# Attention's softmax sums: seven steps of a chunk summed on TensorE

## The chip, the cores and the metric

The kernel runs on one core of a Trainium2 chip. A core has four engines that compute, each with its own queue of instructions: TensorE (PE in the profile; its weight loads are shown apart as PEld), VectorE (DVE), ScalarE (ACT) and GpSimd (POOL). SyncE (SP) issues most DMA transfers. The engines wait for each other through semaphores. TensorE writes its results into PSUM, a memory of banks, and the other engines read them there. The metric is the device time of one execution in microseconds; the time before is the median of three runs.

## What is computed

The reference is a network of two layers on two images of 96 channels and 96 x 96 positions. Layer 0 is a scan with a small feed-forward net, and layer 1 is an attention with another feed-forward net. The change lies in layer 1's attention alone:

```
attn = jnp.einsum('bhdn,bhdm->bhnm', k, q_samp) * scale
attn = jax.nn.softmax(attn, axis=-2)
distribution = jnp.einsum('bhdn,bhnm->bhdm', v, attn)
```

There are 3 heads of 32 channels, n runs over 9216 tokens (keys and values), and m over 2304 cells (queries). The softmax runs over the tokens: for each head and cell, the exponentials of all 9216 scores are summed, and the weighted sum of the values is divided by that sum.

## The kernel before

Layer 1 handles the two images one after the other: a planned stage makes keys, queries and values, `_l1_attention` computes the attention, and a second planned stage makes the output. `_l1_attention` has two arms, chosen by a bound on the scores; in the profile it is the arm without shifted scores, `_l1_packed`, that runs.

`_l1_packed` cuts the 2304 cells into five chunks: four of 480 cells (10 rows of 48) and one of 384. The 9216 tokens are 72 blocks of 128. TensorE's array has 4 strips of 32 rows, and 3 heads fill only three of them, so the fourth strip is given a quarter of the work: 18 of the 72 blocks (`SHARED`), for each of the three heads in turn. What remains is 54 steps for each chunk. In step j, strips 0 to 2 take token block 18 + j of heads 0 to 2, and strip 3 takes block t of head p, where p, t = divmod(j, 18).

One step consists of these pieces:

- Scores (L1311): four matmuls of 32 rows by 128 columns, one for each strip, into two PSUM tiles of two banks (`sc`). There are three such tiles, and a step takes two. The scores of step j + 1 are issued ahead of the values of step j.
- Exponentials (L1315): two ScalarE instructions, each over two strips, into `pr`, of which there are three buffers.
- Values (L1372): four matmuls of 128 rows by 32 columns, which add into a PSUM bank. Strips 0 to 2 write partitions 0 to 95 of the chunk's bank, `main`. Strip 3 writes partitions 96 to 127 of `banks[(m + p) % 2]`, which is the other bank while p is 1.
- Sums (L1380, L1382, L1383, L1385): VectorE adds `pr`, 128 x 4 x 480, into `sums` of the same shape. After 18 steps the fourth strip's part is folded into its head's (L1387), and ScalarE saves its values (L1389).

When a chunk is done, `close` finishes it in three pieces, which are spread over the next chunk. ScalarE first copies the bank (L1325). In step 2 of the next chunk TensorE sums `sums` over the partitions by matmuls with ones (L1328), into the chunk's own bank, and VectorE takes reciprocals (L1332). In step 6 TensorE puts the values back together with the fourth strip's parts (L1336, a matmul of 128 rows, and L1340, one of 32 rows), and VectorE multiplies them into `dist` (L1344). The last chunk's close has no next chunk beside it.

TensorE's order is that of the program (`_in_order`). The other engines' order is left to the scheduler, which puts the reciprocal after the sums of step 3 and the multiplication after those of step 7. An f32 matmul shows as two records of TensorE in the profile, and likewise two weight loads.

Of the kernel before, what the change touches and what calls it, by code (L numbers as in the profile page):

```python
# [8 lines left out]
F32 = mybir.dt.float32  # L9
# [4 lines left out]
ALU = mybir.AluOpType  # L14
# [11 lines left out]
C = 96  # L26
# [17 lines left out]
HEADS = 3  # L44
HD = 32
# [10 lines left out]
def _in_order(k, tc, start, engines=ENGINES):  # L56

    last = {}
    for i in k.nc.cur_bb.bb.instructions[start:]:
        if i.engine in engines:  # L60
            if i.engine in last:
                tc.add_manual_dep(
                    i,
                    last[i.engine].name,
                    mybir.DependencyInfo(
                        mybir.DependencyClass.NoSync, mybir.DependencyReason.DATA
                    ),
                    reason="in_order",
                )
            last[i.engine] = i  # L70
# [1209 lines left out]
SHARED = NTOK // 128 // 4  # L1280


def _l1_packed(k, tc, wk, ps, pa, M):

    nc = k.nc
    qH, kH, vT, dist = M.qH, M.kH, M.vT, M.dist
    steps = NTOK // 128 - SHARED  # L1290
    last = slice(HEADS * HD, (HEADS + 1) * HD)
    chunks = [(r0, min(10, CELLS - r0)) for r0 in range(0, CELLS, 10)]
    banks = [pa.tile([128, 512], F32, tag=f"a{n}", name=f"av{n}", bufs=1) for n in range(2)]
    cells = lambda m: slice(chunks[m][0] * CELLS, (chunks[m][0] + chunks[m][1]) * CELLS)
    q3 = {}

    def load(m, p):
        if m < len(chunks):
            n = chunks[m][1] * CELLS
            q3[m, p] = wk.tile([128, 480], F32, tag="q3", name="q3", bufs=2)  # L1300
            nc.sync.dma_start(q3[m, p][last, :n], qH[p * HD : (p + 1) * HD, cells(m)])

    def scores(m, j):
        n, (p, t) = chunks[m][1] * CELLS, divmod(j, SHARED)
        pr = wk.tile([128, 4, 480], F32, tag="pr", name="pr", bufs=3)
        two = [ps.tile([128, 2, 512], F32, tag="s", name="sc", bufs=3) for _ in range(2)]
        for s in range(4):
            rows = slice(s * HD, (s + 1) * HD)
            k0 = (SHARED + j) * 128 if s < HEADS else (p * SHARED + t) * 128
            q = qH[rows, cells(m)] if s < HEADS else q3[m, p][rows, :n]  # L1310
            nc.tensor.matmul(  # L1311
                two[s // 2][:, s % 2, :n], kH[rows, k0 : k0 + 128], q, start=True, stop=True
            )
        for i in range(2):
            nc.scalar.activation(  # L1315
                pr[:, 2 * i : 2 * i + 2, :n], two[i][:, :, :n], AF.Exp, scale=HD**-0.5
            )
        return pr

    def close(m, av, sums, av3):  # L1320

        n = chunks[m][1] * CELLS
        avs = wk.tile([128, 480], F32, tag="avs", name="avs", bufs=2)
        rden = wk.tile([C, 480], F32, tag="rden", name="rden", bufs=1)
        nc.scalar.copy(avs[:, :n], av[:, :n])  # L1325
        yield
        for hd in range(HEADS):
            nc.tensor.matmul(  # L1328
                av[hd * HD : (hd + 1) * HD, :n], k.ones[:, :HD], sums[:, hd, :n],
                start=True, stop=True,  # L1330
            )
        nc.vector.reciprocal(rden[:, :n], av[:C, :n])  # L1332
        yield
        for hd in range(HEADS):
            rows = slice(hd * HD, (hd + 1) * HD)
            nc.tensor.matmul(  # L1336
                av[rows, :n], k.join[:, rows], avs[:, :n], start=True, stop=hd == HEADS - 1
            )
            if hd < HEADS - 1:
                nc.tensor.matmul(  # L1340
                    av[rows, :n], k.ident[last, last], av3[last, hd, :n], start=False, stop=True
                )
        r0, rows = chunks[m]
        nc.vector.tensor_tensor(  # L1344
            dist[:, 1 + r0 : 1 + r0 + rows, 1 : CELLS + 1],
            av[:C, :n].rearrange("p (r w) -> p r w", w=CELLS),
            rden[:, :n].rearrange("p (r w) -> p r w", w=CELLS),
            ALU.mult,
        )
        yield  # L1350

    start = len(nc.cur_bb.bb.instructions)
    load(0, 0)
    load(0, 1)
    ahead, rest = scores(0, 0), None
    for m in range(len(chunks)):
        n = chunks[m][1] * CELLS
        sums = wk.tile([128, 4, 480], F32, tag="sums", name="sums", bufs=2)
        av3 = wk.tile([128, 2, 480], F32, tag="av3", name="av3", bufs=2)
        for j in range(steps):  # L1360
            p, t = divmod(j, SHARED)
            pr = ahead
            if j + 1 < steps:
                ahead = scores(m, j + 1)
            elif m + 1 < len(chunks):
                ahead = scores(m + 1, 0)
            main, other = banks[m % 2], banks[(m + p) % 2]
            for s in range(4):
                blk, hd = (SHARED + j, s) if s < HEADS else (t, p)
                end = steps if s < HEADS else SHARED  # L1370
                at = j if s < HEADS else t
                nc.tensor.matmul(  # L1372
                    (main if s < HEADS else other)[s * HD : (s + 1) * HD, :n],
                    vT[:, blk, hd, :],
                    pr[:, s, :n],
                    start=at == 0,
                    stop=at == end - 1,
                )
            if j == 0:
                nc.vector.tensor_copy(sums[:, :, :n], pr[:, :, :n])  # L1380
            elif t == 0:
                nc.vector.tensor_tensor(sums[:, :3, :n], sums[:, :3, :n], pr[:, :3, :n], ALU.add)  # L1382
                nc.vector.tensor_copy(sums[:, 3, :n], pr[:, 3, :n])  # L1383
            else:
                nc.vector.tensor_tensor(sums[:, :, :n], sums[:, :, :n], pr[:, :, :n], ALU.add)  # L1385
            if t == SHARED - 1:
                nc.vector.tensor_tensor(sums[:, p, :n], sums[:, p, :n], sums[:, 3, :n], ALU.add)  # L1387
                if p < 2:
                    nc.scalar.copy(av3[last, p, :n], other[last, :n])  # L1389
            if t == 1:  # L1390

                load(m + (p + 2) // 3, (p + 2) % 3) if j > 1 or m else load(0, 2)
            if rest and j in (2, 6):
                next(rest)
        rest = close(m, main, sums, av3)
        next(rest)
    for _ in rest:
        pass
    _in_order(k, tc, start, (mybir.EngineType.PE,))


def _l1_attention(k, tc, M):
# [4 lines left out]
    with ExitStack() as st:  # L1407
# [34 lines left out]
        with cmp.Else():  # L1442
            arm(lambda wk, ps, pa: _l1_packed(k, tc, wk, ps, pa, M), False)
# [363 lines left out]
```

## Time and profile before

| what | value |
| --- | --- |
| time, median of 3 runs | 9239.88 us (9234.12 to 9240.49) |
| profiled execution, its own time | 9236.83 us |
| its span, first to last instruction | 9235.0 us |
| busy: VectorE / TensorE / GpSimd / ScalarE | 8357.2 / 7773.2 / 6272.5 / 6152.4 us |
| attention of the first image | 7129 to 7753 us |
| attention of the second image | 8225 to 8850 us |

The numbers below are from one profiled execution, whose span starts at 0. A group's line gives the code line, engine, operation, output and inputs, shape and count; then the busy time and the mean length of one instruction in ns; then the idle time of the engine just ahead of these instructions and what ended it. Busy time is no measure of a bound by itself, because an engine can be busy while nobody waits for it, and TensorE's records overlap. In attention, windows of 120 us in mid-stage look like this (stretch, its length, busy time and count of TensorE, weight loads, VectorE, ScalarE and GpSimd, then the granted TensorE clock, the DMA share and GB/s):

```profile
7250.00:7370.00 120.00, 119.64 (x840) 36.86 (x836) 114.52 (x59) 95.57 (x106) 0.00 (x0) 1.00 0.01 2
7370.00:7490.00 120.00, 119.63 (x846) 36.75 (x840) 114.78 (x60) 95.51 (x107) 0.00 (x0) 1.00 0.01 3
```

VectorE's busy time leaves a gap of about 0.1 us between two of its instructions where the second waits for a semaphore. TensorE appears busy throughout, which here is the overlap of its records and not a sign that it has no room.

### The profile page before, as it was taken

The page shows a single profiled execution, that of the slowest core. Times are in us where ns is not written, and L with a number is a line of the kernel's source. Part 1 is how long each engine was busy: PE and PEld are TensorE (multiplying, and loading weights), DVE is VectorE, ACT ScalarE, POOL GpSimd, SP SyncE. Part 2 cuts the span into 40 slices and gives each one's busy share as a digit, 9 for nine tenths or more (in the row PEclk, how much of TensorE's full clock was granted, in tenths as well). Part 3 has the DMA queues.
Part 4 walks back from the last instruction along what each step waited for, and adds up shares of the span by engine and source line. Part 5 has one row for each costly group of instructions (what it writes and reads, how often), then busy time and mean ns, then how long its engine had stood idle before and what let it go on. Part 6 is the DMA issues. An engine that isn't in the chain of part 4 may idle for free. (4 is left out here: it accounts for less than half of the span.)

```text
span 9235.0 us, 108247 instructions
## 1 busy us (share of the span) xinstructions
PE 7773.2 (84%) x36625; PEld 3146.3 (34%) x36625; DVE 8357.2 (90%) x6239; ACT 6152.4 (67%) x9970; POOL 6272.5 (68%) x4058
## 2 busy tenths in 40 slices
PE   6888888888888888888888888888857999989998
PEld 3333333333333333333333333333313334543345
DVE  3999999999999999999999999999996998969997
ACT  4666666666666666666666666666645875577755
POOL 4988888888888888888888888888863001210022
PEclk8888888888888888888888888888856999989999
DMA  2444444444444444444444444444431000000000
GB/s 80 131 140 139 140 141 137 136 139 135 134 140 137 134 141 139 139 141 136 138 139 134 135 141 136 136 140 138 137 127 42 3 2 7 20 27 2 2 11 21
DMA packets 335626, 968.69 MB, mean 105 GB/s; under 512 B 50424, under 2 KB 52144, under 8 KB 334768
## 3 DMA queue, kind: packets, MB, share of 16 engines
q1 hardware_dynamic: 335056, 961.64, 32.8%
q8 instruction: 291, 4.77, 0.2%
q14 instruction: 279, 2.29, 0.1%
HBM read 788.04 MB, written 132.17 MB: 100 GB/s over the span
## 5 line engine op out<-in xcount | busy, mean ns | idle before, releaser
L986 POOL TENSOR_TENSOR h<-h,cre 128x864 f32<-128x864 f32 x2048 | 4123.3, 2023 | 806.5 <-DVE h L983 426.7
L983 DVE TENSOR_TENSOR_SCAN h<-dA,bp 128x864 f32<-128x864 f32 x2048 | 4000.0, 1953 | 242.7 <-PE y L995 10.8
L959 ACT ACTIVATE dA<-dlr,A 128x576 f32<-128x576 f32 x3072 | 2156.4, 765 | 1035.0 <-DVE h L983 916.3
L973 DVE TENSOR_TENSOR bp<-dur,B 128x864 f32<-128x864 f32 x2048 | 2174.6, 1062 | 193.4 <-DMA dur<-du_d 11.8
L995 PE MATMUL y<-h,fold 128*32 128x288 f32 x12288 | 2081.1, 592 | 100.3 <-POOL h L986 93.0
L531 PE MATMUL pc<-xin,off 96*96 96x288 f32 x4608 | 1360.2, 427 | 1.6 <-ACT fh L816 1.0
L970 PE MATMUL B<-bt,selb 128*128 128x288 bf16 x2048 | 653.2, 319 | 779.1 <-DVE bp L973 772.2
L1315 ACT ACTIVATE pr<-sc 128x960 f32<-128x960 f32 (+1 forms) x1080 | 955.4, 937 | 255.8 <-DVE sums L1385 144.2
L1385 DVE TENSOR_TENSOR sums<-sums,pr 128x1920 f32<-128x1920 f32 (+1 forms) x510 | 1059.2, 2077 | 58.4 <-ACT pr L1315 7.5
L531 PEld LDWEIGHTS pc<-xin,off 96*96 96x96 f32 x4608 | 743.6, 171 | 575.3 <-issue 281.4
L1466 POOL MEMSET vch<- 96x32 f32 x16 | 2.0, 125 | 1317.4 <-DVE dist L1344 1267.6
L995 PEld LDWEIGHTS y<-h,fold 128*32 128x32 f32 x12288 | 338.9, 116 | 1274.8 <-issue 662.5
L1311 PE MATMUL sc<-qH,kH 32*128 32x480 f32 (+1 forms) x3240 | 708.4, 602 | 9.4 <-DMA q<-qH 9.4
L970 PEld LDWEIGHTS <-selb 128*128 128x128 bf16 x2048 | 205.4, 100 | 1095.1 <-issue 1011.0
L1311 PE MATMUL sc<-q,kH 32*128 32x480 f32 (+1 forms) x1080 | 564.3, 602 | 0.0
L1372 PE MATMUL av<-pr,vT 128*32 128x480 f32 (+1 forms) x4320 | 533.4, 564 | 3.8 <-ACT av L1389 3.5
L705 PE MATMUL pt<-xd,w_dt 96*128 96x288 f32 x768 | 365.7, 573 | 149.7 <-DVE rest L650 88.1
L1311 PEld LDWEIGHTS sc<-qH,kH 32*128 32x128 f32 x3240 | 284.6, 184 | 438.3 <-issue 303.6
L710 ACT ACTIVATE e<-pt,dt_b 128x288 f32<-128x288 f32 x384 | 190.8, 497 | 351.1 <-PE pt L705 341.7
L1539 DVE SCALAR_TENSOR_TENSOR acc<-vch,lepe_w,acc 96x1152 f32<-96x1152 f32 x256 | 406.6, 1588 | 5.0
L1509 POOL TENSOR_TENSOR e<-e,mask 100x384 f32<-100x384 f32 x96 | 146.2, 1544 | 269.3 <-ACT e L1507 269.3
L705 PEld LDWEIGHTS pt<-xd,w_dt 96*128 96x128 f32 x768 | 163.7, 251 | 412.2 <-DVE rest L650 168.0
(249 smaller groups left out, 10476.4 us busy)
## 6 DMA issues: line engine op xcount, KB each, us to landing
cre<-c_d SPq DMA_DIRECT2D x1024, 288.0 KB
dur<-du_d SPq DMA_DIRECT2D x256, 864.0 KB
dlr<-dl_d SPq DMA_DIRECT2D x256, 864.0 KB
x<-xs SPq DMA_DIRECT2D x512, 72.0 KB
du_d<-du SPq DMA_DIRECT2D x128, 288.0 KB
dl_d<-dl SPq DMA_DIRECT2D x128, 288.0 KB
du_d<-du SPq DMA_DIRECT2D x128, 144.0 KB
dl_d<-dl SPq DMA_DIRECT2D x128, 144.0 KB
```

The source lines that it names most:

```text
L531: pe(H2, lambda: nc.tensor.matmul(pc.ap[:C, :H2], k.w_c1[:, ih, tap, oh * C : (oh + 1) * C], xin.ap[:, ih, 3 * c + dy : 3 * c + dy + 3, dx ...
L705: pe(H2, lambda: nc.tensor.matmul(pt.ap[:, :H2], k.w_dt[:, o, m, :], xd.ap[:, cols], start=True, stop=True), ((xd, c),), (pt,), (e, r))
L959: S.op("act", 0.76, lambda blk=blk: nc.scalar.activation(dA.ap[:, :, blk, :], dlr.ap[:, blk, :].rearrange("p (c n) -> p c n", c=2), AF.Exp ...
L970: S.op("pe", 0.3, lambda: nc.tensor.matmul(pB.ap[:, :H2], k.selb[:, kk, i, :], f.bc[o].ap[:, toks], start=True, stop=True), (f.bc[o],), (p ...
L973: S.op("dve", 1.13, lambda: nc.vector.tensor_tensor(bp.ap[:, : NBL * H2].rearrange("p (b n) -> p b n", b=NBL), dur.ap[:, :, toks], pB.ap[: ...
L983: nc.vector.tensor_tensor_scan(hv, dv, bv, 0.0, ALU.mult, ALU.add)
L986: S.op("pool", 2.1, lambda: nc.gpsimd.tensor_tensor(ht.ap, ht.ap, cre.ap[:, toks].unsqueeze(1).to_broadcast([128, NBL, H2]), ALU.mult), (c ...
L995: nc.tensor.matmul(py[c].ap[CB * blk : CB * blk + CB, :H2], k.fold, hv, start=False, stop=(o == 1 and kk == 1 and i == NQ - 1))
L1311: nc.tensor.matmul(two[s // 2][:, s % 2, :n], kH[rows, k0 : k0 + 128], q, start=True, stop=True)
L1315: nc.scalar.activation(pr[:, 2 * i : 2 * i + 2, :n], two[i][:, :, :n], AF.Exp, scale=HD**-0.5)
L1372: nc.tensor.matmul((main if s < HEADS else other)[s * HD : (s + 1) * HD, :n], vT[:, blk, hd, :], pr[:, s, :n], start=at == 0, stop=at == e ...
L1385: nc.vector.tensor_tensor(sums[:, :, :n], sums[:, :, :n], pr[:, :, :n], ALU.add)
```

## The change

In steps 9, 15, 23, 29, 33, 41 and 47 of each chunk VectorE no longer adds strips 0 to 2. Instead TensorE multiplies the exponentials of these three strips by ones, which sums them over the 128 tokens of the block, and adds the result up in partitions 0 to 95 of the bank that the next chunk will use for its values (`side`). VectorE adds only the fourth strip's 480 columns in these steps. After step 47 ScalarE copies the sums from the bank to `part`. At the chunk's close each of the three matmuls by ones is followed by one with a 32 x 32 piece of the identity, which adds `part` to the same partitions.

```diff
+SUMMED = (9, 15, 23, 29, 33, 41, 47)
...
-    def close(m, av, sums, av3):
+    def close(m, av, sums, av3, part):
...
         for hd in range(HEADS):
+            rows = slice(hd * HD, (hd + 1) * HD)
             nc.tensor.matmul(
-                av[hd * HD : (hd + 1) * HD, :n], k.ones[:, :HD], sums[:, hd, :n],
-                start=True, stop=True,
+                av[rows, :n], k.ones[:, :HD], sums[:, hd, :n], start=True, stop=False
+            )
+            nc.tensor.matmul(
+                av[rows, :n], k.ident[rows, rows], part[rows, :n], start=False, stop=True
             )
         nc.vector.reciprocal(rden[:, :n], av[:C, :n])
...
+        part = wk.tile([C, 480], F32, tag="part", name="part", bufs=1)
         for j in range(steps):
...
-            if j == 0:
+            if j in SUMMED:
+                side = banks[(m + 1) % 2]
+                for s in range(HEADS):
+                    nc.tensor.matmul(
+                        side[s * HD : (s + 1) * HD, :n], k.ones[:, :HD], pr[:, s, :n],
+                        start=j == SUMMED[0], stop=j == SUMMED[-1],
+                    )
+                nc.vector.tensor_tensor(sums[:, 3, :n], sums[:, 3, :n], pr[:, 3, :n], ALU.add)
+                if j == SUMMED[-1]:
+                    nc.scalar.copy(part[:, :n], side[:C, :n])
+            elif j == 0:
                 nc.vector.tensor_copy(sums[:, :, :n], pr[:, :, :n])
...
-        rest = close(m, main, sums, av3)
+        rest = close(m, main, sums, av3, part)
```

## The prediction

> **What bounds the kernel now.** I read the page first (busy shares, the chain that ended last, the costly groups), then the windows and the timeline of the two attention stages, then the chain inside one of them. The change touches only attention, which the timeline puts at 7129 to 7753 us (first image) and 8225 to 8850 us (second): some 1,250 of 9235 us.
>
> ```profile
> DVE 29%; PE 14%; issue 2%; ACT 1%; POOL 1%; DVEq 0%; DMA 0%; SPq 0%; POOLq 0%; ACTq 0%
> ...
> L1315 ACT ACTIVATE pr<-sc 128x960 f32<-128x960 f32 (+1 forms) x1080 | 955.4, 937 | 255.8 <-DVE sums L1385 144.2
> L1385 DVE TENSOR_TENSOR sums<-sums,pr 128x1920 f32<-128x1920 f32 (+1 forms) x510 | 1059.2, 2077 | 58.4 <-ACT pr L1315 7.5
> ```
>
> VectorE's running sum of the exponentials (L1385) is busy 1059 us, most of attention, and waits 7.5 us for its input; ScalarE, which makes that input, waits 144 us for L1385 to give a `pr` buffer back. The chain of waits, cut to the middle of a chunk, is that one line (start, length, what):
>
> ```profile
> 7304.48 2.17 DVE sums L1385
> ...
> 7306.74 2.17 DVE sums L1385
> 7308.91 0.03 issue
> 7308.94 0.02 DVEq L1385
> 7308.96 0.04 issue
> 7309.00 2.17 DVE sums L1385
> ```
>
> A step is 2.26 us there, all VectorE's. The question is how far behind TensorE is. That shows where VectorE does not yet hold the ring, right after the first start (TensorE alone, start and length):
>
> ```profile
> 7143.51 1.01 PE L1372 MATMUL av<-pr,vT 128*32 128x480 f32 x8
> 7144.45 0.68 PE L1311 MATMUL sc<-qH,kH 32*128 32x480 f32 x3
> ...
> 7145.47 1.01 PE L1372 MATMUL av<-pr,vT 128*32 128x480 f32 x8
> 7146.41 0.85 PE L1311 MATMUL sc<-qH,kH 32*128 32x480 f32 x3
> 7146.61 0.67 PE L1311 MATMUL sc<-q,kH 32*128 32x480 f32 x1
> ...
> 7147.60 1.01 PE L1372 MATMUL av<-pr,vT 128*32 128x480 f32 x8
> ```
>
> From one value group (L1372) to the next it is 1.96, then 2.13 us, alternating: 0.94 for the values, 1.02 for the scores, and in every second step 0.2 more for the last two score strips, which wait for a score bank that ScalarE still reads. So TensorE and ScalarE together need 2.045 us a step, only 0.22 below VectorE. In the last chunk (384 cells) the same steps take 1.64 and 1.82, mean 1.73, against 1.86.
>
> The third view is a chunk's close, TensorE alone:
>
> ```profile
> 7260.78 0.98 PE L1328 MATMUL av<-sums,ones 128*32 128x480 f32 x6
> 7261.69 0.68 PE L1311 MATMUL sc<-qH,kH 32*128 32x480 f32 x3
> ...
> 7269.76 0.97 PE L1336 MATMUL av<-avs,join 128*32 128x480 f32 x2
> 7270.66 0.99 PE L1340 MATMUL av<-av,ident 32*32 32x480 f32 x2
> 7271.58 0.99 PE L1336 MATMUL av<-avs,join 128*32 128x480 f32 x2
> ```
>
> Three sums by ones (L1328, x6 since an f32 matmul is two records) run beside each other: 0.91 us for all. But where a 128-row matmul and a 32-row identity alternate (L1336, L1340), each one alone takes 0.92.
>
> [...] after a 3.7 us idle the granted clock of 7741 to 7753 is 0.50.
>
> **The change part by part**, one image, against the profiled execution (9236.8 us, span 9235.0, which lies 3.1 below the median of 9239.9).
>
> (a) VectorE, in 7 steps a chunk: an add of 1920 becomes one of 480. L1387 is that form, 0.66; 2.16 - 0.66 = 1.5 us, 10.5 a chunk.
>
> (b) TensorE, in the same steps: three sums by ones after the values, the shape of L1328. Values to scores takes 0.94 without and 1.74 with them (7259.95 to 7261.69), so +0.80; 5.6 a chunk. With 384 columns I estimate 0.64 (0.80 by the column ratio). No new wait ahead of them: they read what the values read, and the bank's last reader (L1344 of the chunk before) ends in step 7 or 8, ahead of step 9.
>
> (c) TensorE, at each close: ones, identity, ones, identity, ones, identity. By the L1336/L1340 row that is 6 x 0.92 = 5.5 in place of 0.80: +4.7. Bounds: +0.8 if the columns ran beside each other, +5.5 if every group were as slow as the slowest.
>
> (d) ScalarE: one copy of 96x480 after step 47, 0.55 by L1389. It waits for the new sums, and the next exponential behind it waits for scores that TensorE issues only after those, about 1.0 us long: hidden, nothing. If that cover were gone, 0.55 a chunk. SP's loads do not move.
>
> Once the 7 adds are gone VectorE needs about 126 - 10.5 = 115 us a chunk and TensorE becomes the bound everywhere. By stretches of steps, from the starts of L1372 in the timeline (chunk 1 as the model of 1 to 3), before and after:
> - 0 to 2: 4.53, then 4.26.
> - 2 to 6, with the first close: 9.0, then 13.7 by (c).
> - 6 to 9, with the second close: 10.5, unchanged.
> - 9 to 17, 2 summed steps: 17.2, then 8 x 2.045 + 2 x 0.80 = 18.0.
> - 17 to 36, 3 summed: 43.5, then 19 x 2.045 + 3 x 0.80 + 0.1 = 41.35 (0.1, an estimate, for the wait at ScalarE's copy L1389).
> - 36 to 54, 2 summed: 41.2, then 18 x 2.045 + 1.6 + 0.2 = 38.65.
> Sum 125.9 before, 126.45 after: +0.5, three times +1.5.
> First chunk, no close: +0.95 - 2.15 - 2.55 = -3.75. Last chunk, 384 cells, with chunk 3's close of 480: stretches 102.75 before; after, 3.5 + 12.4 + 9.6 + 15.1 + 34.9 + 30.9 = 106.4: +3.65.
> At the end VectorE is 2.2 us behind ScalarE now (last `pr` ends 7736.24, its add starts 7738.46). After step 47 it has caught up and loses 0.13 a step for 6 steps, so it is 0.8 behind: -1.5. The last close lies bare: L1328 now takes 1.96 (7740.37 to 7742.33) with the clock falling in it. With TensorE idle only some 2 us before it I expect full clock, 6 x 0.76 = 4.6 (0.92 less 96 columns' share): +2.6. Bounds: at half clock, where L1336 has 1.42 each, 8.5 and so +6.5; if the clock also held through L1336/L1340, 5 x (1.42 - 0.76) = 3.3 would come back, -0.7.
> Sum for an image: -3.75 + 1.5 + 3.65 - 1.5 + 2.6 = +2.5; both images +5. So 9236.8 + 5 = 9242 by the profiled execution, 9244 to 9245 by the median; I take 9244. VectorE's 2 x 48 us of saved adds is nearly all covered by TensorE, which stood 10 us a chunk behind and is given 10.3.
>
> **Rivals.**
> Faster: the closing pairs of different columns run beside each other in spite of the shape. Then (c) costs about 0.9 and not 4.7 at four closes and 2 less at the bare one: 17 us an image, 34 in all, about 9210. For it: the operands are in different columns. Against: L1340 and the following L1336 are too, and show 0.92.
> The change does not do what it says, that is, VectorE stays the bound and its 10.5 a chunk come through in full: 2 x 4.8 x 10.5 = 101 less, 9139. It needs TensorE well under 2.0 us a step; the unblocked step of 1.96 speaks against.
> Slower: TensorE's alternation is lost. Each summed step shifts ScalarE against the score banks (three tiles, two a step). If this makes every step a blocked one (2.13 and 1.82), it costs 0.085 in each of 540 steps, 46 us: 9290. It decides once two steps in three are blocked instead of one in two (15 us on top of the 5). For it: the bound is this very loop. Against: a summed step gives ScalarE 0.8 us to empty its queue, so the following scores should find their banks free.
>
> **How the numbers follow.** A measurement here can tell about 0.2% (18 us) from no change. My case, TensorE takes over at nearly the old pace: 0.70; its own range is 9228 to 9260 (0.5 us a chunk either way is 5, the bare close from -0.7 to +6.5 makes -7 to +8 for two). The closing pairs overlap, 0.12. VectorE stays the bound, 0.02. Lost alternation, or a stall of like size by the 5.5 us close, after which VectorE owes a 3.1 us reciprocal, 0.16. Hence faster 0.14, same 0.70, slower 0.16. The range, widened into both sides, is 9216 to 9270.
>
> **What would show it.** Right: L1315's wait for the sums nearly gone; value groups 2.0 to 2.15 apart with 2.75 to 2.95 at summed steps; six closing groups 0.92 apart; VectorE's adds waiting for ScalarE at most steps; in the chain, TensorE's lines in place of VectorE's. Wrong: closing groups starting within a few ns of each other; summed steps above 3 us; nearly all steps at 2.13; or VectorE still without a pause.

## The result and the profile after

The changed kernel takes 9242.97 us, the median of 12 runs (9240.54 to 9245.44), and the kernel before 9237.44 us beside it (12 runs, 9234.12 to 9240.98). The ratio is 1.0006, with a 95% interval of 0.9997 to 1.0015: the change makes no difference that can be told from none. VectorE has 70 wide additions turned into short ones, and the time stays where it was.

The profile shows that the two kernels get there in different ways. From the page after, the costly groups that answer to those shown of before (line, engine, operation, tiles, shape, count, then busy time and mean length, then the engine's idle time ahead of them and who ended it):

```profile
L1319 ACT ACTIVATE pr<-sc 128x960 f32<-128x960 f32 (+1 forms) x1080 | 954.0, 937 | 255.6 <-PE sc L1315 227.5
L1403 DVE TENSOR_TENSOR sums<-sums,pr 128x1920 f32<-128x1920 f32 (+1 forms) x440 | 913.9, 2077 | 134.3 <-ACT pr L1319 102.6
```

L1319 and L1403 are L1315 and L1385 of before. VectorE's wide sums lost 145 us of busy time (the 70 short adds bring 45 back), and they now wait 103 us for ScalarE where it was 7.5. ScalarE's idle time is the same 256 us as before, but it ended mostly with VectorE's sums (144 us) and now ends with TensorE's scores (228 us). VectorE has gone off the path and TensorE is on it. The chain of waits over the close of a chunk says so line by line (start, length, what):

```profile
7252.78 0.94 PE av L1380 x8
7253.73 1.02 PE sc L1315 x8
7254.74 0.94 PE av L1380 x8
7255.69 0.79 PE av L1333 x2
7256.47 0.92 PE av L1336 x2
7257.39 0.92 PE av L1333 x2
7258.31 0.92 PE av L1336 x2
7259.23 0.92 PE av L1333 x2
7260.15 0.92 PE av L1336 x2
7261.07 1.02 PE sc L1315 x8
```

Every piece is TensorE's. The six groups of the close (L1333 by ones, L1336 by the identity) stand one after the other and take 5.4 us, where three matmuls by ones took 0.91 before. The same chain a few steps on shows a summed step, of values, sums and scores:

```profile
7309.43 0.94 PE av L1380 x8
7310.37 0.80 PE av L1390 x6
7311.17 1.02 PE sc L1315 x8
7312.19 0.94 PE av L1380 x8
7313.13 1.19 PE sc L1315 x8
```

The sums of a summed step (L1390) are 0.80 us, and the steps around them alternate between 1.96 (0.94 + 1.02) and 2.13 us, as they did before where VectorE did not yet hold back the ring of three `pr` buffers. Windows over the same stretches of time as before, with the same columns, show where VectorE's work went:

```profile
7250.00:7370.00 120.00, 119.64 (x882) 31.52 (x876) 103.99 (x59) 94.84 (x107) 0.00 (x0) 1.00 0.01 2
7370.00:7490.00 120.00, 119.64 (x880) 31.76 (x880) 104.97 (x59) 95.22 (x106) 0.00 (x0) 1.00 0.01 3
```

VectorE falls from 114.5 and 114.8 to 104.0 and 105.0 us busy, ten less. TensorE issues 4 to 5% more matmuls in the same time. Its busy time reads 119.6 in both kernels, so that column could not have told who sets the pace.

At the end of an image the close is bare. TensorE's timeline there, before, then after:

```profile
7740.37 1.96 PE L1328 MATMUL av<-sums,ones 128*32 128x384 f32 x6 [3.23 <-DVE sums L1385]
7745.04 1.49 PE L1336 MATMUL av<-avs,join 128*32 128x384 f32 x2 [2.71 <-DVE rden L1332]
7746.46 1.48 PE L1340 MATMUL av<-av,ident 32*32 32x384 f32 x2
```

```profile
7738.57 0.80 PE L1333 MATMUL av<-sums,ones 128*32 128x384 f32 x2 [1.59 <-DVE sums L1403]
7739.30 0.83 PE L1336 MATMUL av<-part,ident 32*32 32x384 f32 x2
7740.06 0.83 PE L1333 MATMUL av<-sums,ones 128*32 128x384 f32 x2
```

TensorE waits 1.59 us for VectorE's last sums instead of 3.23, because VectorE is no longer two microseconds behind. The six groups then run 0.76 apart, at a granted clock of 1.00 (7737 to 7744 us). From the first of them to the reciprocal it is 4.7 us (7738.57 to 7743.27), against 2.07 before (7740.37 to 7742.44).

From the first scores to the end of the last `dist`, attention is 3.7 us longer in the first image and 1.4 in the second. The first two steps run while the clock is still low (granted 0.50 to 0.52 over the first 8 us), and took 1.2 us more in one image and 1.2 less in the other. Without them it is 2.5 us for each image.

### The profile page after: what moved, and what is told of

It reads as the page before. It is cut to its first block, busy times and chain, and to the rows that moved or that the text cites. A ratio compares the mean times of both kernels' runs of the same rounds, so it can differ in the third digit from the quotient of the medians.

```text
span 9238.9 us, 109217 instructions
## 1 busy us (share of the span) xinstructions
PE 7764.9 (84%) x37105; PEld 3096.5 (34%) x37105; DVE 8260.3 (89%) x6239; ACT 6156.3 (67%) x9980; POOL 6269.0 (68%) x4058
## 4 chain that ended last, share of the span: by engine, by line
DVE 61%; PE 26%; issue 5%; ACT 2%; POOL 1%; DVEq 1%; DMA 0%; SPq 0%; POOLq 0%
DVE h L983 34%; DVE bp L973 20%; PE sc L1315 6%; PE av L1380 5%; DVE acc L1557 3%; PE y L995 3%; PE pc L531 3%; DVE rd L1541 1%; PE pp L1573 1%; PE px L603 1%; PE B L970 1%; DVEq L983 1%; PE av L1390 1%; DVE rest L650 1%; POOL h L986 1%
## 5 line engine op out<-in xcount | busy, mean ns | idle before, releaser
L1319 ACT ACTIVATE pr<-sc 128x960 f32<-128x960 f32 (+1 forms) x1080 | 954.0, 937 | 255.6 <-PE sc L1315 227.5
L1403 DVE TENSOR_TENSOR sums<-sums,pr 128x1920 f32<-128x1920 f32 (+1 forms) x440 | 913.9, 2077 | 134.3 <-ACT pr L1319 102.6
L1315 PE MATMUL sc<-qH,kH 32*128 32x480 f32 (+1 forms) x3240 | 622.1, 602 | 10.0 <-DMA q<-qH 10.0
L1315 PE MATMUL sc<-q,kH 32*128 32x480 f32 (+1 forms) x1080 | 564.7, 603 | 0.0
L1315 PEld LDWEIGHTS sc<-qH,kH 32*128 32x128 f32 x3240 | 214.7, 185 | 422.3 <-PE sc L1315 208.5
```

Source lines behind the costliest of these rows:

```text
L1315: nc.tensor.matmul(two[s // 2][:, s % 2, :n], kH[rows, k0 : k0 + 128], q, start=True, stop=True)
L1319: nc.scalar.activation(pr[:, 2 * i : 2 * i + 2, :n], two[i][:, :, :n], AF.Exp, scale=HD**-0.5)
```

## The experiments

All ratios are to the kernel before, which ran beside each group of kernels; its median was 9234.35 us beside `e1_grouped` to `e4_four` and 9235.13 beside `e5_close_only` to `e8_join_before`.

**Is the close slow because of its order?** `e1_grouped` puts the three sums by ones first and the identities after them:

```diff
         for hd in range(HEADS):
             rows = slice(hd * HD, (hd + 1) * HD)
             nc.tensor.matmul(
                 av[rows, :n], k.ones[:, :HD], sums[:, hd, :n], start=True, stop=False
             )
+        for hd in range(HEADS):
+            rows = slice(hd * HD, (hd + 1) * HD)
             nc.tensor.matmul(
```

> The changed kernel with the close's six matmuls in another order: the three sums by ones first, then the three identity pieces. Theory A ([...] six groups of 0.92 us were an effect of the order): ones 0.8 and identities about 0.9 us, 1.7 instead of 5.5 us a close, 3.8 less at four closes and about 3 at the bare one: 18 us an image, 36 in all, so about 9207 us (ratio to before 0.9967). Theory B (a 32-row identity matmul takes 0.92 by itself in any order): 0.8 + 2.8 = 3.6 us a close, 1.9 less at ten closes: about 9224 us. Theory C (the close is covered, and the time has another cause): 9243 us, no change.

Measured: 9205.6 us, ratio 0.9969 (0.9956 to 0.9981). Its close in TensorE's timeline:

```profile
7257.05 0.98 PE L1333 MATMUL av<-sums,ones 128*32 128x480 f32 x6
7257.96 1.00 PE L1338 MATMUL av<-part,ident 32*32 32x480 f32 x6
```

All three identities (x6, two records each) lie in one microsecond. The same six matmuls cost 1.8 us in this order, from the first to the next scores, and 5.4 in the other. Theory A holds, B would have shown 9224, and C 9243.

**Is it the change of shape, or two writers to the same partitions?** `e2_96rows` keeps the alternating order and changes the shape of the identity piece alone:

```diff
-                av[rows, :n], k.ident[rows, rows], part[rows, :n], start=False, stop=True
+                av[rows, :n], k.ident[:C, rows], part[:, :n], start=False, stop=True
```

> The changed kernel in its own order (ones, identity, ones, identity, ones, identity), but each identity piece as 96 rows by 32 columns over the whole of part, which gives the same sum. Theory A [...]: if 96 rows count as the shape of 128 rows, [...] the six run as three columns beside each other, two deep: 1.6 to 1.8 us, about 9207 us as with the grouped order. Theory B (alternating writers of the same partitions, or an accumulation that must end before the next starts, makes them serial): six groups of 0.83 to 0.92 us as before, about 9241 us.

Measured: 9203.81 us, ratio 0.9963 (0.9950 to 0.9977).

```profile
7255.70 1.01 PE L1333 MATMUL av<-sums,ones 128*32 128x480 f32 x6
7256.50 1.01 PE L1336 MATMUL av<-part,ident 96*32 96x480 f32 x6
```

The order in the program is ones, identity, ones, identity, and yet the timeline has all the ones beside each other and then all the identities. With 96 rows instead of 32 the groups no longer stand one after the other, the three columns run beside each other, and the six take 1.7 us up to the scores. Each column still has two writers, one after the other. So these were not what made the close serial; together with `e1_grouped`, where 32 rows are kept and only the order differs, this leaves the change between 128 and 32 rows.

**The seven steps without the close.** `e3_no_ident` drops the three identity matmuls, so that `part` is left out of the sums.

> The changed kernel without the three identity matmuls of the close; it leaves out the addition of part, so the denominators lack the seven steps' sums of strips 0 to 2. It shows the seven summed steps alone. Theory A: the close falls back to 0.8 us, TensorE's chunk to 121.7 us (126.45 less 4.7): 4.7 less at four closes and 2.5 at the bare one, 21 us an image, 43 in all: about 9200 us (ratio 0.9960). If instead the summed steps themselves cost more than the 0.80 us taken, or the close was covered, it stays above 9225 us.

Measured: 9193.36 us, ratio 0.9957 (0.9944 to 0.9971), some 40 us below before. The summed steps alone pay that much.

**The close without the seven steps.** `e5_close_only` is the kernel before, with an identity piece after each matmul by ones. It reads `avs`, since there is no `part`, and so adds wrong terms to the sums; the work is that of the new close.

> The kernel before with the new close's order alone: after each matmul by ones one with a 32x32 piece of the identity (over avs, so it changes the denominators; it adds work and leaves none out). No step is summed on TensorE. It prices the close where VectorE sets the pace. Theory A (the close costs 4.7 us of TensorE, and is only covered as far as VectorE has work in hand): VectorE runs dry for 2 to 3.5 us after the second piece of the close, because the step 2 piece has delayed the scores; with the bare close at half clock (5 to 6.5 more) 13 to 20 us an image, 26 to 40 in all: ratio 1.003 to 1.0045. Rival (TensorE's 10 us of room a chunk cover it wholly): only the bare closes show, 10 to 13 us, ratio 1.0013.

Measured: 9273.43 us, ratio 1.0041 (1.0027 to 1.0055), 38 us above before. This is theory A. VectorE's timeline around the close, of before and of this run, shows where it waits:

```profile
7269.36 6.62 DVE L1385 TENSOR_TENSOR sums<-sums,pr 128x1920 f32<-128x1920 f32 x3
7276.45 2.16 DVE L1385 TENSOR_TENSOR sums<-sums,pr 128x1920 f32<-128x1920 f32 x1 [0.47 <-ACT pr L1315]
7278.52 0.65 DVE L1344 TENSOR_TENSOR dist<-av,rden 96x480 f32<-96x480 f32 x1
7279.09 11.20 DVE L1385 TENSOR_TENSOR sums<-sums,pr 128x1920 f32<-128x1920 f32 x5
```

```profile
7264.78 6.62 DVE L1388 TENSOR_TENSOR sums<-sums,pr 128x1920 f32<-128x1920 f32 x3
7271.87 2.16 DVE L1388 TENSOR_TENSOR sums<-sums,pr 128x1920 f32<-128x1920 f32 x1 [0.47 <-DVE sums L1388]
7274.36 0.66 DVE L1347 TENSOR_TENSOR dist<-av,rden 96x480 f32<-96x480 f32 x1 [0.33 <-PE av L1339]
7277.23 13.47 DVE L1388 TENSOR_TENSOR sums<-sums,pr 128x1920 f32<-128x1920 f32 x6 [2.22 <-ACT pr L1315]
```

The first fence is before, the second this run. The 5.4 us at step 2 use up what VectorE had in hand, and the second piece at step 6 then leaves it dry: 0.33 us until the joins are done, 2.22 us until the next exponentials. From one chunk's `dist` to the next it is 129.1 us instead of 125.9. The two bare closes, 5.6 us longer each from the last values to `dist`, make up 11 of the 38 us, and the eight covered ones the other 27. TensorE had 10 us of room in a chunk on the whole, by the prediction's estimate, but not where the close needs it.

**Who sets the pace in the changed kernel?** `e4_four` takes four summed steps in place of seven:

```diff
-SUMMED = (9, 15, 23, 29, 33, 41, 47)
+SUMMED = (9, 23, 33, 47)
```

> The changed kernel with four summed steps (9, 23, 33, 47) in place of seven, the close unchanged. Theory A (TensorE is the bound of a chunk): three summed steps less are 3 x 0.80 = 2.4 us of TensorE a chunk less, of which a part goes back to VectorE in the longer stretches between summed steps: 1 to 2.4 us a chunk, 10 to 23 in all: 9220 to 9233 us, faster than with seven. Rival (VectorE still sets the pace, the seven steps pay): three adds more of 1.5 us, 4.5 us a chunk, 43 in all: about 9286 us, slower than with seven.

Measured: 9226.71 us, ratio 0.9991 (0.9983 to 0.9999). Taking fewer steps from VectorE makes the kernel faster: four summed steps are some 14 us faster than seven, by the two ratios. With seven, TensorE sets the pace.

**Was TensorE's close on the path before the change?** `e8_join_before` regroups only the second piece of the close, in the kernel before: the three joins first, then the two 32-row matmuls.

```diff
                 av[rows, :n], k.join[:, rows], avs[:, :n], start=True, stop=hd == HEADS - 1
             )
-            if hd < HEADS - 1:
-                nc.tensor.matmul(
-                    av[rows, :n], k.ident[last, last], av3[last, hd, :n], start=False, stop=True
-                )
+        for hd in range(HEADS - 1):
+            rows = slice(hd * HD, (hd + 1) * HD)
+            nc.tensor.matmul(
+                av[rows, :n], k.ident[last, last], av3[last, hd, :n], start=False, stop=True
+            )
```

> The kernel before with the joins regrouped alone. Theory A (before the change VectorE sets the pace and TensorE's close is covered): nothing at the hidden closes, about 4 us at each bare one, 8 in all: ratio 0.9991. Rival (TensorE's close is on the path before the change too): 2.7 us at four closes more an image, 30 in all: ratio 0.9968.

Measured: 9228.45 us, ratio 0.9993 (0.9984 to 1.0001). The interval takes in both 1 and the 0.9991 expected, and shuts out the rival's 0.9968. TensorE's second piece shows both groups, three and two matmuls, beside each other:

```profile
7268.13 0.98 PE L1336 MATMUL av<-avs,join 128*32 128x480 f32 x6
7269.04 0.99 PE L1341 MATMUL av<-av,ident 32*32 32x480 f32 x4
```

The piece is 2.7 us shorter, and still a chunk stays at 125.9 us between its `dist` and the next. At the bare closes the gain is 4.3 and 4.8 us.

**The same edit where TensorE sets the pace, and a better balance.** `e6_both` is `e2_96rows` with the joins regrouped, and `e7_five` the same with five summed steps, 9, 20, 29, 38 and 47.

> Seven summed steps, the identity pieces of 96 rows as in the run before, and the close's second piece regrouped too: the three 128-row join matmuls first, then the two 32-row ones. Theory A (changes of shape): five serial groups of 0.92 become two of 0.92, 2.7 us less at four hidden closes and about 4 at the bare one at half clock: 15 us an image, 30 in all below the 96-row run: about 9174 us, ratio 0.9934. Rival (the two 32-row matmuls share rows 96 to 127 and stay serial behind the joins): three groups, 1.8 less each: about 9184 us.

> The same with five summed steps (9, 20, 29, 38, 47). Theory A: with both closes short TensorE needs 119.8 us a chunk at seven and VectorE 115.4; five steps give TensorE 118.2 and VectorE 118.4, the crossing: 1.5 us a chunk less, 14 to 16 in all: about 9159 us, ratio 0.9917. Rival (the ring of three buffers holds too little, so that stretches of nine to eleven steps between summed ones are paced by VectorE): no gain on seven, 9174 us or more.

Measured: 9175.61 us, ratio 0.9937 (0.9923 to 0.9951), and 9161.23 us, ratio 0.9919 (0.9905 to 0.9932). The interval of `e6_both` takes in its rival's 9184 us too; the trace decides against the rival, since the two 32-row matmuls (x4, two records each) run beside each other:

```profile
7264.83 0.98 PE L1343 MATMUL av<-avs,join 128*32 128x480 f32 x6
7265.74 0.99 PE L1348 MATMUL av<-av,ident 32*32 32x480 f32 x4
```

The regrouping that was worth some 7 us under VectorE, where it paid at the bare closes alone, is worth 24 by the ratios, 28 by the medians, under TensorE. There a covered chunk goes from 122.9 us (`e2_96rows`) to 120.1, and with five summed steps to 118.4. `e7_five` beats the kernels before and after the change, by 74 us against before, and each of its five runs is faster than each run of `e6_both`. The waits of `e7_five` in its first attention stage, by groups:

```profile
L1404 DVE TENSOR_TENSOR sums<-sums,pr 128x1920 f32<-128x1920 f32 (+1 forms) x230 | 477.6, 2077 | 27.5 <-ACT pr L1319 4.8 <-DVE sums L1404 0.5
L1319 ACT ACTIVATE pr<-sc 128x960 f32<-128x960 f32 (+1 forms) x540 | 477.2, 937 | 93.0 <-PE sc L1315 73.3 <-DVE sums L1404 5.8 <-DVE sums L1402 3.2
```

VectorE waits only 4.8 us for the exponentials, and ScalarE only 5.8 for VectorE's sums. So VectorE hardly waits and hardly holds anyone up: it is nearly in balance with TensorE. What is left over is ScalarE's wait for TensorE's scores, 73 us, and in the chain of waits from 7280 to 7300 us TensorE has 90%.

## Why the prediction was right

It said that VectorE's saved time would be covered by TensorE, 9244 us, and it came out at 9243. The term that decided was (c), read from a row that belonged to another piece of work, the alternating joins L1336 and L1340.

- **(a) VectorE, 1.5 us a summed step.** Held: the short add has a median of 658 ns, and the windows show ten microseconds less in 120. The "2 x 48 us" of saved adds is a slip; the prediction's own 101 us for both images is the sum of its terms.
- **(b) TensorE, 0.80 us a summed step.** Held to the hundredth in the chain. No matmul of L1390 waited for another engine.
- **(c) the close, 5.5 for 0.80.** Held, 5.4, and `e1_grouped` and `e2_96rows` show the cause. The faster rival, in which columns go beside each other in spite of the shape, fell for the kernel as written. Its price was about right: where order or shape let the columns run beside each other, the time was 9204 to 9206, with 9210 foretold.
- **(d) ScalarE's copy hidden.** Held: nobody waited for L1396, and ScalarE did not idle before it.
- **The stretches of a chunk.** The predicted values for steps 0 to 2, 2 to 6, 6 to 9, 9 to 17, 17 to 36 and 36 to 54 were 4.26, 13.7, 10.5, 18.0, 41.35 and 38.65. Chunk 2 shows 4.15, 13.57, 10.51, 17.98, 41.60 and 38.80. The only term that was sized too small is what ScalarE's copies (L1407) cost when the fourth strip changes heads, taken as 0.1 and 0.2, where by difference 0.35 came in each stretch. (The terms written out for the last stretch add up to 38.61, not 38.65.) The errors cancel to 0.15 us a chunk.
- **The end of an image.** TensorE's wait for VectorE came down by 1.6 us (1.5 foretold), and the bare first piece took 2.6 more, as taken. In the first image the clock held through that piece (granted 1.00 from 7737 to 7744) and was at half by the joins (0.50 from 7745, 1.42 a group), as assumed; neither bound was reached. That some 2 us of idle time leave the full clock was the author's estimate, from one longer idle stretch of before, and its length was misread. TensorE's idle time ahead of L1328 there is 3.23 us, as its timeline above shows, and not the prediction's 3.7, which counts from the start of the last values. After the change a shorter idle stretch, 2.71 us ahead of the joins, came before a fall too. In the first image the clock fell inside it (granted 0.81 from 7744 to 7745), in the second about its end (1.00 from 8840 to 8843, 0.85 from 8843 to 8844, 0.50 after that), and there the first join took 1.09. So it is not shown how safe the 1.59 us ahead of the first piece were.
- **The sum.** 2.5 us for each image, after the uneven start is taken out: the predicted figure. That it fits so well is partly luck. From its third step on the first chunk gained 3.2 us where 3.75 was foretold, the last lost 3.0 where 3.65 was, and the two misses cancel.
- **The slower rival, lost alternation.** It fell: after a summed step the steps read 2.13, 1.96, 2.13, 1.96. **VectorE stays the bound** fell with `e4_four`.
- **A sign that came only in part.** VectorE's adds were to wait for ScalarE at most steps. They did so at 132 of 440, nearly all in the one or two steps after a close or a summed step. In an ordinary step VectorE (2.26 us) is still slower than TensorE (2.045), so it soon falls behind again and works without a pause until the next summed step.

One sentence of the prediction needs more than it said. It has TensorE "10 us a chunk behind" and "given 10.3", as if the room were a sum. `e5_close_only` shows that it is not: with those 10 us still free, the new close alone costs 38 us over the kernel, 27 of them where other work covers it. The summed steps alone gain 40. Together they would give -2, and the chip shows about +5, because the steps move the pace to TensorE and every microsecond of its close then counts in full: with the summed steps a covered chunk takes 126.6 us with the identities and 122.0 without (`e3_no_ident`), 4.6 more, where it was 3.2 more without the summed steps.

## What to carry to other kernels

When work moves from the engine that sets the pace to the next one, price everything that comes along with it on the new engine, the clean-up included: here the moved sums were worth 40 us and the small matmuls that fold them back in took it all. Look at the shapes in a row of TensorE's small matmuls: the six of this close took 5.4 us alternating between 128 and 32 rows, 1.8 us grouped by shape, and 1.7 us with the 32 rows widened to 96. And once the pace has moved, try the count again, since fewer moved steps with both pieces of the close made cheap gave the fastest of the kernels tried here.

## What the runs showed of the hardware

A row of matmuls that alternates between 128 and 96 rows ran with its columns beside each other (1.7 us for six), where one that alternates between 128 and 32 rows ran one group after the other (5.4 us). Other row counts weren't tried, and why the one row is serial is not shown. And in `e2_96rows` matmuls of one column strip started ahead of those of another strip that come earlier in the kernel's text: all three by ones lie within 1.01 us (7255.70 to 7256.71), where one alone took 0.97 in the changed kernel, and no identity starts before 7256.50, though one stands between each two. Whether the engine or the compiler orders them so wasn't tried.
